# Seven half-size products for the second neighbour stage of a graph network's second layer, with the norms among the counts' products

## The chip, the core and the metric

The kernel runs on one core of a Trainium2 chip. The time is the device time of one execution in microseconds (us). PE is the tensor engine, DVE the vector engine, ACT the scalar engine, POOL the GpSimd engine; SP only issues DMAs here.

## What is computed

A graph of 625 nodes with 1024 features and 10000 edges goes through two layers. Layer 1 adds a two-step neighbour network (GraphSAGE) and a linear attention to x, then an attention with experts. The part that the change touches is the last line of the first block:

```python
def _sage_layer(h, edge_src, edge_dst, deg_inv, W_self, W_neigh, b):
    msg = h[edge_src]
    agg = segment_sum(msg, edge_dst, num_segments=h.shape[0])
    mean = agg * deg_inv[:, None]
    return h @ W_self + mean @ W_neigh + b
...
h = relu(_sage_layer(xn, src, dst, deg_inv, W_self0, W_neigh0, b0))
out = _sage_layer(h, src, dst, deg_inv, W_self1, W_neigh1, b1)
...
x = x + out + linear_attention(xn) @ L1_Wo + L1_bo
x = x + attention_and_experts(layernorm(x))
```

Everything is in f32. Written for the rows of one tile of nodes, the second step is x += h W_self1 + o L1_Wo + D^-1 C (h W_neigh1) + b. Here o is the linear attention's output before its last product, C the matrix of edge counts between nodes and D the in-degrees.

## The kernel before

The nodes are five tiles of 125 rows (`NT` = 5, `P` = 125), the features eight chunks of 128 (`KC` = 8). `hT` (two tiles of four chunks) and `oT` hold h and o with features on partitions, so that a matmul takes a 128x125 piece of them as its weights and streams 512 columns of a weight matrix. `group(dst, pairs)` (L137) sums a list of such matmuls in PSUM.

The order of every engine's work is written out by hand: `do(prep, pe, after)` emits first the `after` steps of the call before, then the PE work `pe`. Thus the evacuation of a product stands in the program behind the PE work that follows it, and each engine goes through its own list in that order.

Weights come in 1 MB tiles of 8 KB a partition from a pool of six buffers (`wpool`, tag "w"). `Half` loads one half of a matrix's columns (512) in two such tiles; `Quarter` loads 256 columns of a block in one. The loads stand in SP's queue in program order, and each waits until the buffer that it takes has been read for the last time.

The first step of the network (`quarter`, called as `p1` to `p3`) is already computed by Winograd's form of Strassen's scheme. A product of 2x2 blocks then takes seven block products instead of eight, with sums of blocks before (S1 to S4 of the left side, the mixes `third`, `second`, `first`, `fourth` of the weights) and after (u and u3). There [xn mean] is one side and [W_self0; W_neigh0] the other, in two quarters of 256 columns.

The second step is plain. For a half c of the columns, `neighbours(c)` makes z = h W_neigh1 for the five tiles (eight matmuls of 512 columns each, `pz`), and `split` writes it as a high part (rounded to fp32r, by ACT) and the rest (DVE). `last_of(t, c)` then makes, for a tile t, a group of sixteen matmuls (h W_self1 + o L1_Wo) and a group of ten counts' products in fp32r (C times both parts of z, five tiles of nodes each). DVE adds the two groups to x. The order is `neighbours(0)`, `last_of(0..4, 0)`, `neighbours(1)`, `last_of(0..4, 1)`.

Behind `last_of(t, 1)` stand `norm_rows(t - 1)`, the normalisation of a finished row of x (statistics, two square roots, `xs`), and `turn_rows(nxT, t - 2, 0)`, which transposes `xs` on PE and scales it into `nxT`. Tiles 3 and 4 are turned among the first key and query products of the next attention (`keys`, `q0`).

Of the kernel before, what the change touches and what calls it, by code (L numbers as in the profile page):

```python
# [20 lines left out]
NT = 5  # L21
# [32 lines left out]
def attempt(ctx: ExitStack, tc: tile.TileContext, w: dict, out: bass.AP, shifted: bool):  # L54
# [8 lines left out]
    def ps1(name):  # L63
        pool, n = psums[-1]
        return pool.tile([128, 512], FP, tag="ps1", name=name, bufs=n)
# [47 lines left out]
    class Half:  # L113


        def __init__(self, pool, src, c, tag="w", padded=None, now=True):
            v = src.rearrange("(k p) n -> p k n", p=128)
            self.parts = []

            def load():  # L120
                i = len(self.parts)
                t = pool.tile([128, 4, 512], FP, tag=tag, name="w", padded_shape=padded)
                self.parts.append(t)
                return nc.sync.dma_start(out=t, in_=v[:, 4 * i:4 * i + 4, c * 512:(c + 1) * 512])

            self.load = lambda: behind(load(), latest["pe"])
            if now:
                load()
                load()
# [4 lines left out]
    def group(dst, pairs):  # L134

        for i, (lhsT, rhs) in enumerate(pairs):
            made = nc.tensor.matmul(dst, lhsT=lhsT, rhs=rhs, start=(i == 0), stop=(i == len(pairs) - 1))  # L137
        latest["pe"] = made.ins.name

    class Quarter:  # L140


        def __init__(self, lo, *parts):
            self.tiles = {}
            self.source = {name: [(src, k, lo + 512 * (name[1] == "2")) for src, k in parts[int(name[0]) - 1]]
                           for name in ("11", "12", "21", "22")}

        def room(self, name):
            self.tiles[name] = wpool.tile([128, KC, 256], FP, tag="w", name="wq" + name)

        def load(self, *names):
            for name in names:
                self.room(name)
                at = 0
                for src, k, lo in self.source[name]:
                    n = k.stop - k.start
                    nc.sync.dma_start(out=self.tiles[name][:, at:at + n, :],
                                      in_=w[src].rearrange("(k p) n -> p k n", p=128)[:, k, lo:lo + 256])
                    at += n

        def mix(self, dst, a, b, op):
# [14 lines left out]
    def add(dst, a, b):  # L176
        nc.vector.tensor_tensor(dst, a, b, op=ALU.add)
# [19 lines left out]
    def nodes(t):  # L197
        return slice(t * P, (t + 1) * P)
# [1032 lines left out]
    def split(src, high, low):  # L1231

        nc.scalar.activation(high, src, AF.Copy)
        if not shifted:
            nc.vector.tensor_tensor(low, src, high.bitcast(FP), op=ALU.subtract)
# [38 lines left out]
    meanT = []  # L1274

    every = slice(0, KC)
    quarters = [Quarter(256 * i, [("W_self0", every)], [("W_neigh0", every)]) for i in range(2)]
    quarters[0].room("2")
    quarters[0].load("12", "21", "11", "22")
    for k in range(KC):  # L1280
# [38 lines left out]
    def four(f):  # L1319
        for j in range(2):  # L1320
            f(slice(4 * j, 4 * j + 4), meanT[j])
# [17 lines left out]
    def quarter(i):  # L1339
        q = quarters[i]  # L1340
        kept = {}
        u = spool.tile([128, 2, HN], FP, tag="u", name="u", bufs=2)
        u3 = spool.tile([128, 2, HN], FP, tag="u", name="u3", bufs=2)

        def product(name, right, after):
            def pe():
                kept[0] = ps2("pw")
                for a in range(2):
                    wt = q.tiles[name]
                    group(kept[0][:, a, :HN], [(wt[:, k, a * 128:(a + 1) * 128], right[k]) for k in range(KC)])  # L1350

            return lambda: do(None, pe, lambda: after(kept[0][:, :, :HN]))

        def done(c, h, a, b):
            dst = hT[c][:, 2 * i:2 * i + 2, h]
            add(dst, a, b)
            for a in range(2):
                m = 4 * c + 2 * i + a
                nc.scalar.activation(dst[:, a, :], dst[:, a, :], AF.Relu, bias=b0_t[:, m:m + 1])

        def both(p):
            done(1, tail, p, u3)
            add(u, p, u)

        return [product("11", A11, lambda p: nc.scalar.activation(u, p, AF.Copy)),
                product("21", A12, lambda p: done(0, head, p, u)),
                product("2", S2k, lambda p: add(u, p, u)),
                product("12", S3k, lambda p: add(u3, p, u)),
                product("21", A22, lambda p: done(0, tail, p, u3)),
                product("11", S1k, both),  # L1370
                product("22", S4k, lambda p: done(1, head, p, u))]

    now, then = quarters
    then.load("12")
    p1, p2, p6, p7, p4, p5, p3 = quarter(0)
    four(sum1)
    four(sum2)
    p1()
    p2()
    now.first()  # L1380
    four(sum3)
    p6()
    now.fourth()
    four(sum4)
    then.load("11")
    p7()
    then.load("22")
    p4()
    then.load("21")
    p5()  # L1390
    then.third()
    p3()
    then.room("2")
    p1, p2, p6, p7, p4, p5, p3 = quarter(1)
    p1()
    then.second()
    p2()
    then.first()
    p6()
    then.fourth()  # L1400
    nc.vector.tensor_tensor(b_t[0], b_t[0], b_t[1], op=ALU.add)
    p7()
    for t in range(2):
        nc.vector.tensor_tensor(x[:, t, :], x[:, t, :], b_t[0][:P], op=ALU.add)
    p4()
    for t in range(2, NT):
        nc.vector.tensor_tensor(x[:, t, :], x[:, t, :], b_t[0][:P], op=ALU.add)
    p5()
    p3()
    z, ws, wo = [], [], []  # L1410

    def neighbours(c):

        zc = big.tile([P, 2, NT, 512], NUM, tag="big", name="z")
        z.append(zc)
        wn1 = Half(wpool, w["W_neigh1"], c)
        ws.append(Half(wpool, w["W_self1"], c))
        wo.append(Half(wpool, w["L1_Wo"], c))
        for t in range(NT):
            def pe():  # L1420
                hold["pz"] = ps1("pz")
                group(hold["pz"][:P], [(hT[k // 4][:, k % 4, nodes(t)], wn1(k)) for k in range(KC)])

            def after(t=t):
                split(hold["pz"][:P], zc[:, 0, t, :], zc[:, 1, t, :])

            do(None, pe, after)

    neighbours(0)
    seven.close()  # L1430


# [26 lines left out]
    def norm_rows(t):  # L1459

        st = pool.tile([P, 2, 6], FP, tag="st", name="st", bufs=2)
        for h in range(2):
            nc.vector.bn_stats(st[:, h, :], x[:, t, h * 512:(h + 1) * 512])
        nc.vector.bn_aggr(mv2[:, t, :], st)
        rs, rr = rs2[:, t:t + 1], r1[:, t:t + 1]
        nc.scalar.activation(rs, mv2[:, t, 1:2], AF.Sqrt, bias=eps_ln[:P], scale=1.0)
        nc.vector.reciprocal(rs, rs)
        nc.vector.scalar_tensor_tensor(rr, mv2[:, t, 1:2], rs, rs, op0=ALU.mult, op1=ALU.mult)
        nc.scalar.activation(rr, rr, AF.Sqrt, bias=eps_6[:P], scale=1.0)
        nc.vector.reciprocal(rr, rr)  # L1470
        nc.vector.tensor_tensor(rr, rr, rs, op=ALU.mult)
        xs = hold["xs", t] = pool.tile([P, D], FP, tag="xs", name="xs", bufs=2)
        nc.vector.tensor_scalar(xs, x[:, t, :], mv2[:, t, 0:1], rr, op0=ALU.subtract, op1=ALU.mult)
# [2 lines left out]
        xs = hold.pop(("xs", t))  # L1476
        do(None, lambda: transpose_in(T, t, xs, lambda dst, src, h: by_gain(dst, src, which, h, P)))

    def last_of(t, c):
        def pe():  # L1480
            p = hold["px"] = ps2("px3")
            group(p[:P, 0, :], [(hT[k // 4][:, k % 4, nodes(t)], ws[c](k)) for k in range(KC)]
                  + [(oT[:, k, nodes(t)], wo[c](k)) for k in range(KC)])
            group(p[:P, 1, :], [(CTr[:, s, nodes(t)], z[c][:, i, s, :]) for i in range(1 if shifted else 2)
                                for s in range(NT)])

        def after():
            xc = x[:, t, c * 512:(c + 1) * 512]
            nc.vector.tensor_tensor(xc, hold["px"][:P, 0, :], xc, op=ALU.add)
            nc.vector.scalar_tensor_tensor(xc, hold["px"][:P, 1, :], dinvT[:, t:t + 1], xc,  # L1490
                                           op0=ALU.mult, op1=ALU.add)

        do(None, pe, after)

    for t in range(NT):
        last_of(t, 0)
    neighbours(1)
    for t in range(NT):
        last_of(t, 1)
        if t:  # L1500
            norm_rows(t - 1)
        if t > 1:
            turn_rows(nxT, t - 2, 0)


    kvc = mid([128, 2 * NP + NT * 256], "kvc")
# [36 lines left out]
                      kcT[:, a, :]) for a in range(2)]  # L1543
    q0 = [query(0, a) for a in range(2)]
    keys[0](0)
    turn_rows(nxT, NT - 2, 0)
    norm_rows(NT - 1)
    keys[1](0)
    q0[0](0)
    turn_rows(nxT, NT - 1, 0)  # L1550
    for t in range(3):
        value(t)
    keys[0](1)
# [639 lines left out]
```

## Time and profile before

| | us |
|---|---|
| median of 3 runs (2128.26 to 2129.67) | 2129.18 |
| the profiled execution, its own time | 2152.51 |
| its span, first to last instruction | 2150.7 |
| first `neighbours` matmul starts | 915.60 |
| first `last_of` matmul starts | 949.93 |
| second pass of `last_of` starts | 1064.51 |
| first key product of the next attention starts | 1148.79 |

PE is busy 2065.9 us of the span (96%), DVE 800.0 (37%), ACT 200.4 (9%), POOL 302.7 (14%). In a profile's row of a group, "x160" counts records: an f32 matmul is two records, an fp32r one is one. The first number behind the bar is the busy time of the group in us with overlaps counted once, the second the mean duration of one record in ns, and the last the idle time of the engine just before the group, with what ended it. Since matmuls overlap in the pipeline, the mean duration is longer than the time that one takes from its successor.

### The profile page before, as it was taken

The page shows a single profiled execution, that of the slowest core. Times are in us where ns is not written, and L with a number is a line of the kernel's source. Part 1 is how long each engine was busy: PE and PEld are TensorE (multiplying, and loading weights), DVE is VectorE, ACT ScalarE, POOL GpSimd, SP SyncE. Part 2 cuts the span into 40 slices and gives each one's busy share as a digit, 9 for nine tenths or more (in the row PEclk, how much of TensorE's full clock was granted, in tenths as well). Part 3 has the DMA queues.
Part 4 walks back from the last instruction along what each step waited for, and adds up shares of the span by engine and source line. Part 5 has one row for each costly group of instructions (what it writes and reads, how often), then busy time and mean ns, then how long its engine had stood idle before and what let it go on. Part 6 is the DMA issues. An engine that isn't in the chain of part 4 may idle for free. (4 is left out here: it accounts for less than half of the span.)

```text
span 2150.7 us, 17267 instructions
## 1 busy us (share of the span) xinstructions
PE 2065.9 (96%) x6806; PEld 1175.4 (55%) x6806; DVE 800.0 (37%) x1290; ACT 200.4 (9%) x369; POOL 302.7 (14%) x321
## 2 busy tenths in 40 slices
PE   8999999599899999999999999999999999999998
PEld 6555475255445787744456776457644444444443
DVE  5775568467532673210022234256311111111012
ACT  2100010012211100000000111111000000000000
POOL 1666656500000000100000000110000000000011
PEclk9999999799999999999999999999999999999999
DMA  7523254080122112410203201122589889987832
GB/s 217 201 91 108 79 178 136 22 229 24 39 88 79 39 40 73 148 64 16 101 0 108 79 1 39 30 79 98 197 327 329 299 298 329 329 315 265 305 130 83
DMA packets 156244, 301.61 MB, mean 140 GB/s; under 512 B 12539, under 2 KB 42114, under 8 KB 156150
## 3 DMA queue, kind: packets, MB, share of 16 engines
q1 hardware_dynamic: 135580, 251.50, 33.3%
q0 software_dynamic: 15584, 38.66, 5.7%
q10 hardware_dynamic: 4986, 10.22, 1.5%
q8 instruction: 57, 0.93, 0.2%
q14 instruction: 37, 0.30, 0.0%
HBM read 277.49 MB, written 22.84 MB: 140 GB/s over the span
## 5 line engine op out<-in xcount | busy, mean ns | idle before, releaser
L137 PE MATMUL pu<-w,xgT 128*128 128x512 f32 x768 | 333.9, 593 | 2.6 <-DVE xgT L1440 2.6
L137 PEld LDWEIGHTS pu<-w,xgT 128*128 128x128 f32 x768 | 144.0, 190 | 175.5 <-issue 172.2
L137 PE MATMUL pyb<-w,hb 128*128 128x512 f32 x384 | 174.3, 598 | 2.4 <-ACT yb L105 2.1
L137 PE MATMUL pk<-w,xnT 128*125 128x512 f32 x320 | 141.3, 593 | 3.9 <-ACT xnT L1104 2.2
L137 PE MATMUL pq<-xnT,w 128*128 128x313 f32 x512 | 139.2, 431 | 3.9 <-DVE v L332 3.9
L137 PE MATMUL pv<-w,xnT 128*125 128x512 f32 x320 | 140.8, 593 | 0.9 <-DVE x L986 0.9
L2027 DVE TENSOR_TENSOR su<-pu,su 128x512 f32<-128x512 f32 x24 | 16.6, 691 | 313.9 <-ACT su L2026 313.9
L137 PEld LDWEIGHTS pq<-xnT,w 128*128 128x128 f32 x512 | 97.9, 192 | 43.0 <-DVE v L332 4.7
L137 PEld LDWEIGHTS pyb<-w,hb 128*128 128x128 f32 x384 | 69.8, 189 | 90.9 <-issue 74.8
L805 PE MATMUL px<-w,oT 128*125 128x512 f32 x160 | 74.1, 619 | 27.7 <-DMA table<-es,at 22.5
L137 PEld LDWEIGHTS pk<-w,xnT 128*125 128x125 f32 x320 | 59.2, 187 | 75.6 <-issue 72.4
L137 PEld LDWEIGHTS pv<-w,xnT 128*125 128x125 f32 x320 | 59.4, 188 | 73.5 <-issue 71.2
L680 POOL DMA_INDIRECT table<-es,at x79 | 85.7, 1085 | 58.9 <-issue 35.0
L660 POOL DMA_INDIRECT ga<-xl_d,si x79 | 79.5, 1006 | 54.3 <-issue 25.9
L2010 POOL DMA_INDIRECT xg<-rows_d,slots x12 | 11.6, 970 | 507.9 <-PE pxg L2017 454.7
L660 POOL DMA_INDIRECT gb<-xr_d,di x79 | 77.2, 977 | 24.1 <-issue 22.9
L137 PE MATMUL px<-w,hT 128*125 128x512 f32 x160 | 70.3, 592 | 0.0
L137 PE MATMUL px<-w,oT 128*125 128x512 f32 x160 | 70.3, 592 | 0.0
L137 PE MATMUL pX<-w,aT 128*125 128x512 f32 x160 | 69.3, 592 | 0.0
L137 PE MATMUL pz<-w,hT 128*125 128x512 f32 x160 | 69.0, 592 | 0.0
L137 PE MATMUL pq<-nxT,w 128*128 128x313 f32 x256 | 68.7, 426 | 0.0
L137 PE MATMUL ph<-S,wq 128*128 128x313 f32 x256 | 68.7, 427 | 0.0
(385 smaller groups left out, 2535.5 us busy)
## 6 DMA issues: line engine op xcount, KB each, us to landing
w<-in_eW_dram SPq DMA_DIRECT2D x144, 1024.0 KB
w<-in_L_Wk_dram SPq DMA_DIRECT2D x8, 1024.0 KB
w<-in_L_Wv_dram SPq DMA_DIRECT2D x8, 1024.0 KB
w<-in_L_Wq_dram SPq DMA_DIRECT2D x8, 1024.0 KB
w<-in_L_Wo_dram SPq DMA_DIRECT2D x8, 1024.0 KB
wq<-in_sW_dram SPq DMA_DIRECT2D x16, 512.0 KB
table<-none SPq DMA_DIRECT2D x1, 6160.0 KB
y_d<-yb ACTq DMA_DIRECT2D x12, 512.0 KB
```

The costliest lines, as they stand in the source:

```text
L137: made = nc.tensor.matmul(dst, lhsT=lhsT, rhs=rhs, start=(i == 0), stop=(i == len(pairs) - 1))
L660: got = nc.gpsimd.indirect_dma_start(out=ab[g][side][0:p, j, :], out_offset=None, in_=src[:, :], in_offset=bass.IndirectOffsetOnAxis(ap=ix ...
L680: put = nc.gpsimd.indirect_dma_start(out=table[:, :], out_offset=bass.IndirectOffsetOnAxis(ap=at[0:p, lo + j:lo + j + 1], axis=0), in_=es[ ...
L805: made = nc.tensor.matmul(hold["px", t][:P, c, :], lhsT=oT[:, k, nodes(t)], rhs=wo[c](k), start=(k == 0), stop=(k == KC - 1 and keep is no ...
L2010: nc.gpsimd.indirect_dma_start(out=xg, out_offset=None, in_=rows_d[:, :], in_offset=bass.IndirectOffsetOnAxis(ap=slots[:, b:b + 1], axis=0))
L2027: nc.vector.tensor_tensor(su, pu[:, 0, :], su, op=ALU.mult)
```

## The change

The second step is remade in three parts.

1. `seven_products` is the old order of the seven products as a function, called four times: twice for the first step as before, and twice for the self and attention products of tiles 0 to 3. In these, [h o] is one side (tokens 0 to 249 and 250 to 499 as its two rows of blocks) and [W_self1; L1_Wo] the other, in quarters of 256 columns. Every product has two tiles of 125 tokens and eight chunks. Results are added to x by DVE.
2. z for tiles 0 to 3 is made by seven products too (`z_products`): h is split into two halves of its features, and the blocks of W_neigh1 are 512 by 512. The fifth tile's z is made by plain products (`z_last`).
3. The fifth tile's own self and attention products (`last_tile`) are plain, from W_self1 and L1_Wo loaded again in halves; `oT4` is a copy of o's last tile, since z takes oT's buffer. They stand among the counts' products (`of_neighbours`, now both halves of the columns of a tile together) and the norms and turns. Tile 4 comes before tiles 2 and 3.

The bias additions to x, which stood between products of the first step, stand there still.

```diff
+    quarters = [Quarter(256 * i, [(a, every)], [(b, every)]) for a, b in (("W_self0", "W_neigh0"), ("W_self1", "L1_Wo"))
+                for i in range(2)] + [Quarter(0, [("W_neigh1", front)], [("W_neigh1", back)], n=512)]
+
+    def seven_products(i, p1, p2, p6, p7, p4, p5, p3, between={}):
+        now, then = quarters[i], quarters[i + 1] if i + 1 < len(quarters) else None
...
+        if then:
+            then.load("12")
+        p1()
+        if i:
+            now.second()
+        other(1)
+        p2()
+        now.first()
+        other(2)
+        p6()
+        now.fourth()
+        other(6)
+        if then:
+            then.load("11")
+        p7()
+        other(7)
+        if then:
+            then.load("22")
+        p4()
+        other(4)
+        if then:
+            then.load("21")
+        p5()
+        if then and then.n == 256:
+            then.third()
+        other(5)
+        p3()
+        if then:
+            then.room("2")
...
-    z, ws, wo = [], [], []
-    def neighbours(c):
...
+    def on_tokens(name, left, wt, n, parts, after):
+        def pe():
+            p = hold[name] = ps2(name)
+            for j in range(2):
+                dst = p[:P, j, :] if n == 512 else p[:P, 0, 256 * j:256 * j + 256]
+                group(dst, [(left(k)[:, j * P:(j + 1) * P], wt()[:, k, :]) for k in range(parts)])
...
+    def rows_quarter(i):
...
+        return [product("11", h_(early), lambda p: nc.scalar.activation(u, p, AF.Copy)),
+                product("21", o_(early), lambda p: plus(at(0, 0), p, u)),
+                product("2", S_(S2), lambda p: add(u, p, u)),
+                product("12", S_(S3), p7),
+                product("21", o_(late4), lambda p: plus(at(0, 2), p)),
+                product("11", S_(S1), p5),
+                product("22", S_(S4), lambda p: plus(at(1, 0), p, u))]
...
+    seven_products(2, *rows_quarter(0), {1: [lambda: by_four(by_sum[0]), lambda: by_four(by_sum[1])],
+                                         2: [lambda: by_four(by_sum[2])], 6: [lambda: by_four(by_sum[3])]})
+    seven_products(3, *rows_quarter(1))
...
-    def last_of(t, c):
...
+    def z_last(c):
...
+    def z_products():
...
+        def done(c, rows, a, b):
+            got = pool.tile([P, 2, 512], FP, tag="zt", name="zt", bufs=1)
+            add(got, a, b)
+            split(got, z[c][:, 0, rows:rows + 2, :], z[c][:, 1, rows:rows + 2, :])
...
+    def of_neighbours(t):
         def pe():
             p = hold["px"] = ps2("px3")
-            group(p[:P, 0, :], [(hT[k // 4][:, k % 4, nodes(t)], ws[c](k)) for k in range(KC)]
-                  + [(oT[:, k, nodes(t)], wo[c](k)) for k in range(KC)])
-            group(p[:P, 1, :], [(CTr[:, s, nodes(t)], z[c][:, i, s, :]) for i in range(1 if shifted else 2)
-                                for s in range(NT)])
+            for c in range(2):
+                group(p[:P, c, :], [(CTr[:, s, nodes(t)], z[c][:, i, s, :]) for i in range(1 if shifted else 2)
+                                    for s in range(NT)])
...
-    for t in range(NT):
-        last_of(t, 0)
-    neighbours(1)
-    for t in range(NT):
-        last_of(t, 1)
-        if t:
-            norm_rows(t - 1)
-        if t > 1:
-            turn_rows(nxT, t - 2, 0)
+    def last_tile(c):
+        ws, wo = (Half(wpool, w[name], c) for name in ("W_self1", "L1_Wo"))
...
+    z_last(1)
+    wn1.third()
+    p1, p2, p6, p7, p4, p5, p3 = z_products()
+    p1()
+    wn1.second()
+    z_last(0)
...
+    p2()
+    wn1.first()
...
+    p6()
+    wn1.fourth()
+    p7()
+    p4()
+    final = [last_tile(0)]
+    p5()
+    p3()
+    final.append(last_tile(1))
+    of_neighbours(0)
+    of_neighbours(1)
+    norm_rows(0)
+    final[0]()
+    norm_rows(1)
+    of_neighbours(4)
+    turn_rows(nxT, 0, 0)
+    of_neighbours(2)
+    turn_rows(nxT, 1, 0)
+    norm_rows(2)
+    final[1]()
+    turn_rows(nxT, 2, 0)
+    of_neighbours(3)
+    norm_rows(4)
...
     keys[0](0)
-    turn_rows(nxT, NT - 2, 0)
-    norm_rows(NT - 1)
+    norm_rows(3)
+    turn_rows(nxT, 4, 0)
     keys[1](0)
     q0[0](0)
-    turn_rows(nxT, NT - 1, 0)
+    turn_rows(nxT, 3, 0)
```

More of the change, by code (lines that the diff above doesn't have):

```diff
@@ L140, in attempt, with __init__ @@
     class Quarter:
-        def __init__(self, lo, *parts):
+        def __init__(self, lo, *parts, n=256):
             self.tiles = {}
+            self.n = n
             self.source = {name: [(src, k, lo + 512 * (name[1] == "2")) for src, k in parts[int(name[0]) - 1]]
@@ L148, in room @@
         def room(self, name):
-            self.tiles[name] = wpool.tile([128, KC, 256], FP, tag="w", name="wq" + name)
+            self.tiles[name] = wpool.tile([128, 2048 // self.n, self.n], FP, tag="w",
+                                          name="wq" + name)
         def load(self, *names):
@@ L157, in load @@
                     nc.sync.dma_start(out=self.tiles[name][:, at:at + n, :],
-                                      in_=w[src].rearrange("(k p) n -> p k n", p=128)[:, k, lo:lo + 256])
+                                      in_=w[src].rearrange("(k p) n -> p k n", p=128)[:, k, lo:lo + self.n])
                     at += n
@@ L1276, in attempt, with other @@
     every = slice(0, KC)
-    quarters = [Quarter(256 * i, [("W_self0", every)], [("W_neigh0", every)]) for i in range(2)]
+    front, back = slice(0, 4), slice(4, KC)
+    quarters = [Quarter(256 * i, [(a, every)], [(b, every)]) for a, b in (("W_self0", "W_neigh0"), ("W_self1", "L1_Wo"))
+                for i in range(2)] + [Quarter(0, [("W_neigh1", front)], [("W_neigh1", back)], n=512)]
+    def seven_products(i, p1, p2, p6, p7, p4, p5, p3, between={}):
+        now, then = quarters[i], quarters[i + 1] if i + 1 < len(quarters) else None
+        def other(name):
+            for f in between.get(name, ()):
+                f()
+        if then:
[27 more added lines that the diff above has]
+            then.room("2")
     quarters[0].room("2")
@@ L1371, in quarter, with biases @@
                 product("22", S4k, lambda p: done(1, head, p, u))]
-    now, then = quarters
-    then.load("12")
-    p1, p2, p6, p7, p4, p5, p3 = quarter(0)
+    def biases(*ts):
+        if 0 in ts:
+            add(b_t[0], b_t[0], b_t[1])
+        for t in ts:
+            add(x[:, t, :], x[:, t, :], b_t[0][:P])
     four(sum1)
     four(sum2)
[L1378 to L1407, printed above, removed]
@@ L1408, in attempt @@
-    p5()
-    p3()
-    z, ws, wo = [], [], []
-    def neighbours(c):
[L1414 to L1418, printed above, removed]
-        for t in range(NT):
[L1420 to L1427, printed above, removed]
@@ L1429, in attempt @@
-    neighbours(0)
+    seven_products(0, *quarter(0), {2: [lambda: four(sum3)], 6: [lambda: four(sum4)]})
+    seven_products(1, *quarter(1), {6: [lambda: biases(0, 1)], 7: [lambda: biases(2, 3, 4)]})
+    seven.close()
+    seven = ExitStack()
+    spool = seven.enter_context(tc.tile_pool(name="rows", bufs=1, reuse_waits="tile"))
+    early, late4 = slice(0, 2 * P), slice(2 * P, 4 * P)
+    S1, S2 = (mid([128, KC, 2 * P], name) for name in ("S1", "S2"))
+    S3, S4 = (spool.tile([128, KC, 2 * P], FP, name=name) for name in ("S3", "S4"))
@@ new lines, in sub, with by_four, done @@
+    def sub(dst, a, b):
+        nc.vector.tensor_tensor(dst, a, b, op=ALU.subtract)
+    def by_four(f):
+        for j in range(2):
+            k = slice(4 * j, 4 * j + 4)
+            f(k, hT[j], oT[:, k, :])
+    def on_tokens(name, left, wt, n, parts, after):
+        def pe():
+            p = hold[name] = ps2(name)
+            for j in range(2):
+                dst = p[:P, j, :] if n == 512 else p[:P, 0, 256 * j:256 * j + 256]
+                group(dst, [(left(k)[:, j * P:(j + 1) * P], wt()[:, k, :]) for k in range(parts)])
+        def done():
+            p = hold[name]
+            after(p[:P] if n == 512 else p[:P, 0, :].rearrange("p (j n) -> p j n", j=2))
+        return lambda: do(None, pe, done)
@@ new lines, in rows_quarter, with at, plus, product @@
+    def rows_quarter(i):
+        q = quarters[2 + i]
+        u, u3 = (spool.tile([P, 2, 256], FP, tag="u", name=name, bufs=2) for name in ("u", "u3"))
+        def at(c, rows):
+            return x[:, rows:rows + 2, c * 512 + 256 * i:c * 512 + 256 * i + 256]
+        def plus(dst, *parts):
+            for part in parts:
+                add(dst, dst, part)
+        def product(name, left, after):
+            return on_tokens("pl", left, lambda: q.tiles[name], 256, KC, after)
+        def h_(tokens):
+            return lambda k: hT[k // 4][:, k % 4, tokens]
+        def o_(tokens):
+            return lambda k: oT[:, k, tokens]
+        def S_(S):
+            return lambda k: S[:, k, :]
+        def p7(p):
+            add(u3, p, u)
+            plus(at(0, 2), u3)
+        def p5(p):
+            plus(at(1, 2), p, u3)
+            add(u, p, u)
+        return [product("11", h_(early), lambda p: nc.scalar.activation(u, p, AF.Copy)),
[5 more added lines that the diff above has]
+                product("22", S_(S4), lambda p: plus(at(1, 0), p, u))]
@@ new lines, in attempt @@
+    by_sum = [lambda k, h, o: add(S1[:, k, :], h[:, :, late4], o[:, :, late4]),
+              lambda k, h, o: sub(S2[:, k, :], S1[:, k, :], h[:, :, early]),
+              lambda k, h, o: sub(S3[:, k, :], h[:, :, early], h[:, :, late4]),
+              lambda k, h, o: sub(S4[:, k, :], o[:, :, early], S2[:, k, :])]
+    seven_products(2, *rows_quarter(0), {1: [lambda: by_four(by_sum[0]), lambda: by_four(by_sum[1])],
+                                         2: [lambda: by_four(by_sum[2])], 6: [lambda: by_four(by_sum[3])]})
@@ L1477, in turn_rows, with pe @@
         do(None, lambda: transpose_in(T, t, xs, lambda dst, src, h: by_gain(dst, src, which, h, P)))
-    def last_of(t, c):
+    oT4 = pool.tile([128, KC, P], FP, name="oT4")
+    nc.scalar.activation(oT4, oT[:, :, nodes(4)], AF.Copy)
+    z = [big.tile([P, 2, NT, 512], NUM, tag="big", name="z") for c in range(2)]
+    S12, S34 = (mid([128, 2, 4, 2 * P], name) for name in ("S12", "S34"))
+    S1, S2, S3, S4 = (S[:, i] for S in (S12, S34) for i in range(2))
+    wn1 = quarters[4]
+    def z_last(c):
+        def pe():
+            hold["pz"] = ps1("pz")
+            group(hold["pz"][:P], [(hT[k // 4][:, k % 4, nodes(4)], wn1.tiles[f"{1 + k // 4}{1 + c}"][:, k % 4, :])
+                                   for k in range(KC)])
+        do(None, pe, lambda: split(hold["pz"][:P], z[c][:, 0, 4, :], z[c][:, 1, 4, :]))
@@ new lines, in z_products, with product, p5 @@
+    def z_products():
+        u, u3 = (pool.tile([P, D], FP, tag="xs", name=name, bufs=2).rearrange("p (j n) -> p j n", j=2)
+                 for name in ("u", "u3"))
+        def product(name, left, after):
+            return on_tokens("pz2", lambda k: left[:, k, :], lambda: wn1.tiles[name], 512, 4, after)
+        def done(c, rows, a, b):
+            got = pool.tile([P, 2, 512], FP, tag="zt", name="zt", bufs=1)
+            add(got, a, b)
+            split(got, z[c][:, 0, rows:rows + 2, :], z[c][:, 1, rows:rows + 2, :])
+        def p5(p):
+            done(1, 2, p, u3)
+            add(u, p, u)
+        return [product("11", hT[0][:, :, early], lambda p: nc.scalar.activation(u, p, AF.Copy)),
+                product("21", hT[1][:, :, early], lambda p: done(0, 0, p, u)),
+                product("2", S2, lambda p: add(u, p, u)),
+                product("12", S3, lambda p: add(u3, p, u)),
+                product("21", hT[1][:, :, late4], lambda p: done(0, 2, p, u3)),
+                product("11", S1, p5),
+                product("22", S4, lambda p: done(1, 0, p, u))]
@@ L1487, in after @@
         def after():
[L1488 to L1491, printed above, removed]
+            xt = x[:, t, :].rearrange("p (c n) -> p c n", c=2)
+            nc.vector.scalar_tensor_tensor(xt, hold["px"][:P], dinvT[:, t:t + 1], xt, op0=ALU.mult, op1=ALU.add)
         do(None, pe, after)
-    for t in range(NT):
-        last_of(t, 0)
@@ L1497, in attempt, with now, pe @@
-    neighbours(1)
-    for t in range(NT):
-        last_of(t, 1)
-        if t:
-            norm_rows(t - 1)
-        if t > 1:
-            turn_rows(nxT, t - 2, 0)
+    def last_tile(c):
+        ws, wo = (Half(wpool, w[name], c) for name in ("W_self1", "L1_Wo"))
+        def now():
+            def pe():
+                hold["pr"] = ps2("pr")[:, 0, :]
+                group(hold["pr"][:P], [(hT[k // 4][:, k % 4, nodes(4)], ws(k)) for k in range(KC)]
+                      + [(oT4[:, k, :], wo(k)) for k in range(KC)])
+            xc = x[:, 4, c * 512:(c + 1) * 512]
+            do(None, pe, lambda: add(xc, hold["pr"][:P], xc))
+        return now
@@ new lines, in attempt @@
+    add(S1, hT[0][:, :, late4], hT[1][:, :, late4])
+    sub(S2, S1, hT[0][:, :, early])
+    z_last(1)
[4 more added lines that the diff above has]
+    z_last(0)
+    sub(S3, hT[0][:, :, early], hT[0][:, :, late4])
+    p2()
+    wn1.first()
+    sub(S4, hT[1][:, :, early], S2)
+    p6()
[8 more added lines that the diff above has]
+    of_neighbours(1)
```

## The prediction

> **What bounds the kernel now.** I read the page's first two sections, then the waits of the tensor engine (PE) in the stretch that the change touches, then that stretch's groups and timeline.
>
> ```profile
> span 2150.7 us, 17267 instructions
> ...
> PE 2065.9 (96%) x6806; PEld 1175.4 (55%) x6806; DVE 800.0 (37%) x1290; ACT 200.4 (9%) x369; POOL 302.7 (14%) x321
> ...
> PEclk9999999799999999999999999999999999999999
> ```
>
> PE works 96% of the span. The stretch is 780 to 1210 us, at granted clock 1.00 in every window that I asked for, so microseconds taken from PE there are microseconds of the run if nothing new makes PE wait. It has two waits today:
>
> ```profile
> engine line waited for: us in total, times, longest us
> PE pkc L137 <- DVE nxT L1440: 1.3, 1, 1.3
> PE pvc L137 <- DVE nxT L1440: 0.3, 1, 0.3
> ```
>
> So the change is worth the difference in PE work, plus or minus waits. The groups of the stretch (780 to 1205 us) and four rows of its timeline give the prices:
>
> ```profile
> L137 PE MATMUL px<-w,hT 128*125 128x512 f32 x160 | 70.3, 592 | 0.0
> L137 PE MATMUL px<-w,oT 128*125 128x512 f32 x160 | 70.3, 592 | 0.0
> L137 PE MATMUL pz<-w,hT 128*125 128x512 f32 x160 | 69.0, 592 | 0.0
> L162 DVE TENSOR_TENSOR wq<-wq,wq 128x2048 f32<-128x2048 f32 x8 | 18.3, 2284 | 7.5 <-PE pw L137 7.5
> L137 PE MATMUL pvc<-wvc,nxT 128*125 128x256 f32 x80 | 17.7, 380 | 0.3 <-DVE nxT L1440 0.3
> L1324 DVE TENSOR_TENSOR S<-xnT,meanT 128x1252 f32<-128x1252 f32 x2 | 2.8, 1454 | 0.0
> ```
>
> ```profile
> 1163.76 10.62 PE L137 MATMUL pvc<-wvc,nxT 128*125 128x256 f32 x48 [0.34 <-DVE nxT L1440]
> 1174.22 0.95 PE L137 MATMUL pkc<-nxT,wkc 128*128 128x313 f32 x3
> 1195.31 7.07 PE L137 MATMUL pvc<-wvc,nxT 128*125 128x256 f32 x32
> 1202.21 0.95 PE L137 MATMUL psc<-qT,kvc 128*125 128x313 f32 x3
> ```
>
> A single matmul's 592 or 380 ns overlaps its neighbours; the price is start to start. Each f32 matmul stands as two records. At 512 columns, a tile's eight `pz` matmuls (16 records) start 6.87 us apart (the copies of z stand at 922.66 and 929.53): 0.429 us a record. At 256 columns, (1202.21 - 1195.31)/32 = 0.2156 and (1174.22 - 1163.76)/48 = 0.2179; I take 0.2165. A tile of `last_of` takes 16.04 us (1064.51 to 1080.54): 32 x 0.429 = 13.73 leaves 2.31 for ten records of counts, 0.231 each.
>
> **The change part by part.**
> *Self and attention products of tiles 0 to 3.* Removed: 4 tiles x 2 halves x 16 matmuls = 256 records of 512 columns, 256 x 0.429 = 109.8 us. Added: two quarters x 7 products x 2 tiles x 8 matmuls = 448 records of 256 columns, 448 x 0.2165 = 97.0 us. Gain 12.8.
> A rule speaks against this step. The Trainium skill, "TensorE: Matmul & The Clock Gate", section "Back-to-back issue gap", says that in a stream of weight loads and matmuls "the per-MM spacing is set by *both* ops"; it gives 81 ns for 128-column pairs against about 56 for the matmul alone. Adding those 25 ns to a 256-column pass (107 + 2.5) is 134 ns, 268 a two-pass record: 448 x 0.268 = 120 us, and the gain turns into a loss of 10 (an estimate from that page). The row of this trace has the same operands in kind (a 128x125 load for every 256-column matmul) at 0.2165, so the 188 ns load is covered. I take the row.
>
> *Neighbour products.* Removed: 160 `pz` records. Added: 7 products x 2 tiles x 4 matmuls x 2 = 112, and the fifth tile's plain 32. 144 x 0.429 = 61.8 against 68.6. Gain 6.9.
>
> *The fifth tile's plain products and the counts' products.* 64 records of 512 columns and 100 of counts stay as many; they only move. Gain 0, from -0.5 to +0.5 for changes of kind between neighbours.
>
> *Vector engine (DVE).* For each self quarter: four weight mixes at 2.28, and 11 additions of 512 columns, no dearer than the 0.69 of `x<-px,x`. The four sums are made once, in eight halves of 1000 columns; at the 1.454/1252 of L1324 that is 1.16 each. Together 2 x (9.1 + 7.6) + 9.3 = 43 us beside 97 of PE. The neighbour stage: 9.1 of mixes, 4.6 of sums, 1.4 for the fifth tile, and 11 passes of 1024 columns at the 1.22 of L986, some 28 us beside 62. I laid them out by product (6.9 us long in both stages): first self product from 0, the last hT addition ends at 1.1, the weight sum at 3.4, S1 at 5.8, S2 at 8.1; S2 and the sum are wanted at 13.8. The hT chunks that the last W0 product finishes (k 6 and 7) are through ACT at 1.8 and 2.3; the new first product reaches them at 2.6 and 3.0. Cost 0; if the cover is gone, the 0.8 us margin of k 6 is the first to break. The 14 evacuations lag by no more than one product, with three PSUM pairs in turn.
>
> *Loads.* 20 MB instead of 12: eight 256-column quarters of W_self1 and L1_Wo, four parts of W_neigh1, eight parts for the fifth tile. Each on SP's queue waits for a buffer: quarter "11" for the third product of the stage before, "22" for the fourth, "21" for the fifth. A 256-column load today: issued at 822.96, bytes until 827.3, so 4.4 us; a 512-column one is alike:
>
> ```profile
> 856.72 0.37 SPq L124 DMA_DIRECT2D w<-in_W_neigh_dram  x1
> ```
>
> ```profile
> 858.00:859.00 1.00, 1.00 (x6) 0.71 (x5) 1.00 (x1) 0.57 (x2) 0.00 (x0) 1.00 0.91 178
> 859.00:860.00 1.00, 1.00 (x6) 0.71 (x5) 0.74 (x1) 0.00 (x0) 0.00 (x0) 1.00 1.06 412
> 860.00:861.00 1.00, 1.00 (x5) 0.71 (x4) 0.00 (x0) 0.00 (x0) 0.00 (x0) 1.00 1.02 397
> 861.00:862.00 1.00, 1.00 (x5) 0.76 (x4) 0.00 (x0) 0.00 (x0) 0.00 (x0) 1.00 0.11 39
> ```
>
> The last two columns are the DMA share and GB/s. "21" is wanted three products (20.7 us) after its issue, "11" four; "22" is the tightest: its mix stands on DVE one product (6.9 us) later, ahead of the next evacuation, and DVE would hold that up by what the load is late. The fifth tile's last two parts are issued while its first half runs, over 20 us before their use. POOL's zero fill of y_d (bytes from 898 to 915 today) moves behind the fourth product of the second self quarter; W_neigh1's "22" is issued at the same moment and has 24 us until its use, "21" one product later with 31. Cost 0; were these the full 17 us late they would still be in time.
>
> *Neighbours to counts.* `last_of` began on old z; now the first counts' products want the z that the last product has just made: addition 1.22, ACT copy some 1.05, subtraction 1.22 in a row. PE reaches the high part after ten records, at 2.3 us, and it is there at 2.6; the low part is wanted five records on, at 3.8, ready at 3.9. Cost 0.4, with bounds 0 and 4 (none of the chain hidden).
>
> *Norms among the counts' products.* Tiles run 0, 1, fifth c=0, 4, 2, fifth c=1, 3. A norm takes 3.9 us on DVE from its statistics to xs (1154.92 to 1158.79); counted from the first counts' product, norms of tiles 0, 1, 2, 4, 3 end at about 10, 16, 40, 55 and 60, and their turns are due on PE at 28, 34, 48, 58 and 68. `keys[0](0)` no longer follows a turn directly: tile 2's nxT is written by 51, and 4.6 us of tile 3's counts' products put the keys at 54. The 1.3 us wait goes; the 0.3 stays. Gain 1.3, bounds -2 and 1.3.
>
> Sum: 12.8 + 6.9 + 1.3 - 0.4 = 20.6 us. The profiled execution took 2152.5 (span 2150.7), so 2131.9 there. It is 23 us slower than the median; the stretch ran at full clock, so I take the same microseconds off the median: 2129.2 - 20.6 = 2108.6.
>
> **The rivals.**
> *Small waits eat part of it.* 21 products with evacuations, mixes and sums in one DVE order: a stall of 0.5 us at each costs 10 and gives 2119. For: the order is written by hand, and DVE stands at the head of its queue waiting for loads and products. Against: today's stage of the same pattern has none:
>
> ```profile
> 797.00:865.00 68.00, 68.00 (x262) 48.99 (x261) 26.31 (x21) 4.71 (x9) 0.00 (x0) 1.00 0.19 62
> ```
>
> There PE is busy 68.00 of 68.00 with DVE at 26.31. New products last 6.9 us where those last 8.4, so the load on DVE is a little higher. 0.13.
> *Slower: the weight load shows.* If a load that changes for every 256-column matmul were only half covered, a record would cost 0.2165 + 0.094 = 0.31, the self stage 139.1 instead of 109.8, and the run 2129.2 + 29.3 - 6.9 - 1.3 + 0.4 = 2150.7. It decides at (20.6/448 = 0.046 more) 0.262 us a record. For: the quoted rule, and 188 ns of load under 216 of matmul is a thin cover. Against: 80 records of the same form, no idle but the 0.3. 0.04.
> *Nothing left.* The self stage neither gains nor loses (0.245 a record) and a few waits of 7 us eat the rest: 2129. For it only the two rivals together. 0.03.
> *The gain is larger.* The smaller pitch (0.2156 throughout), no wait at the counts: 2107.8; anything lower needs a change outside the stretch, where the instruction order is the same. 0.03 for under 2104.
>
> **How the numbers follow.** Forecast 0.77, rivals 0.13, 0.04, 0.03, 0.03. The predicted time is the forecast's, 2109. The range goes from 2104 (below the smaller pitch by the spread of runs and some luck) to 2115 (the counts' chain uncovered, 4, and the key wait's bound); half of the small-wait cases lie above it. 0.2% is 4.3 us, about what a measurement of this kernel can tell from no change. Faster by more: 0.93. Within: 0.03. Slower by more: 0.04.
>
> **What would show it.** Groups `pl` with 448 records at some 97 us busy (0.2165 each, mean near 380 ns), `pz2` and `pz` together 144; no wait of PE in the self and neighbour stages above 0.5 us, one of about 0.4 on z before the first counts' products, no `pkc` wait on nxT. From the end of the last W0 product to the first `pkc` about 212 us against 232 (915.60 to 1147.5). I am wrong if `pl` starts are more than 0.23 apart, if PE waits in total over 4 us there on wq, S or z, or if time changes outside.

## The result, and the profile after

The changed kernel took 2112.11 us (median of 6 runs, 2106.05 to 2118.55) against 2130.6 before (6 runs, 2128.26 to 2132.94): ratio 0.9915, 95% interval 0.9895 to 0.9935. That is 18.5 us less. Timed again among the experiments it took 2109.12 against 2131.18, ratio 0.9897 (0.9878 to 0.9916), 22.1 us less. The forecast was 20.6 less. The first interval stands for 14 to 22 us, the second for 18 to 26. The runs' spread is wider than the differences that matter here, so the working below is checked in the profiles, where a stretch of a few hundred microseconds repeats within some tenths.

From the page of the changed kernel, the rows shown of the one before:

```profile
span 2109.1 us, 17713 instructions
...
PE 2037.1 (97%) x6982; PEld 1207.8 (57%) x6982; DVE 855.6 (41%) x1326; ACT 203.1 (10%) x369; POOL 303.0 (14%) x321
...
PEclk9999999799999999999999999999999999999999
```

The two profiled spans differ by 41.6 us, twice what the timed runs do. One difference of the two traces tells why: the first product of the network's first step, where nothing has been changed yet, starts at 797.46 in the trace before and at 777.1 here, and from 773.0 to 778.0 in the eight kernels of the experiments. So 20.4 us of the 41.6 belong to that one execution of the kernel before, and to the front of the kernel. In that front PE was idle for 14.5 us that the list of waits puts down to "issue", that is, to nothing that the profile shows; the nine profiles of the changed kernel and its variants have 1.9 us of it at most. What it came from stays open. From that product to the end, 1353.2 us have become 1332.0.

The waits of PE from the first new product on (890 to 1180 us):

```profile
engine line waited for: us in total, times, longest us
PE pvc L137 <- DVE nxT L1511: 0.3, 1, 0.3
```

The key products' 1.3 us wait is gone, and no product of the two new stages is in the list. PE's groups between 890 and 1110 us (records, busy us, mean ns):

```profile
L137 PE MATMUL pl<-wq,S 128*125 128x256 f32 x256 | 55.9, 379 | 0.0
L137 PE MATMUL pz<-wq,hT 128*125 128x512 f32 x80 | 34.7, 592 | 0.0
L137 PE MATMUL pl<-wq,oT 128*125 128x256 f32 x128 | 28.3, 379 | 0.0
L137 PE MATMUL pz<-wq,S 128*125 128x512 f32 x64 | 27.8, 592 | 0.0
L137 PE MATMUL px<-z,CT 125*125 125x512 f32 x100 | 25.1, 405 | 0.1
L137 PE MATMUL pl<-wq,hT 128*125 128x256 f32 x64 | 14.1, 379 | 0.0
```

`pl` has 448 records and `pz` (which takes in `pz2`; the trace leaves a name's number out) 144. And the windows from the first self product to z, to the counts' products, to the first key product (columns: length, busy time of PE, weight loads, DVE, ACT, POOL, granted clock, DMA share, GB/s):

```profile
895.30:991.90 96.60, 96.60 (x449) 84.02 (x448) 41.12 (x38) 3.13 (x5) 7.52 (x12) 1.00 0.33 115
991.90:1053.30 61.40, 61.40 (x144) 26.83 (x144) 24.81 (x19) 5.39 (x6) 0.66 (x2) 1.00 0.24 86
1053.30:1107.40 54.10, 54.00 (x190) 32.99 (x189) 23.87 (x46) 4.70 (x10) 0.00 (x0) 1.00 0.52 174
```

The edges of these windows are rounded. Measured from start to start the three are 96.69, 61.40 and 54.06 us, 212.15 in all. In the kernel before, the same work stands between the first `neighbours` matmul and the first key product:

```profile
915.60:1148.79 233.19, 231.89 (x605) 111.03 (x603) 36.80 (x69) 10.61 (x21) 0.62 (x1) 1.00 0.17 59
```

The stretch gives 21.0 us, the whole of the gain within 0.2.

### The profile page after: what moved, and what is told of

It reads as the page before. It is cut to its first block, busy times and chain, and to the rows that moved or that the text cites. A ratio compares the mean times of both kernels' runs of the same rounds, so it can differ in the third digit from the quotient of the medians.

```text
span 2109.1 us, 17713 instructions
## 1 busy us (share of the span) xinstructions
PE 2037.1 (97%) x6982; PEld 1207.8 (57%) x6982; DVE 855.6 (41%) x1326; ACT 203.1 (10%) x369; POOL 303.0 (14%) x321
## 5 line engine op out<-in xcount | busy, mean ns | idle before, releaser
L807 PE MATMUL px<-w,oT 128*125 128x512 f32 x160 | 71.7, 606 | 30.9 <-DMA table<-es,at 27.8
L807 PEld LDWEIGHTS px<-w,oT 128*125 128x125 f32 x160 | 30.3, 192 | 69.9 <-issue 36.3
L164 DVE TENSOR_TENSOR wq<-wq,wq 128x2048 f32<-128x2048 f32 x28 | 63.9, 2283 | 12.8 <-PE pw L137 7.5
L398 DVE RECIPROCAL z<-z 128x626 f32<-128x626 f32 x16 | 65.1, 4066 | 0.6
```

The lines of the kernel that those rows point to most:

```text
L164: nc.vector.tensor_tensor(self.tiles[dst], self.tiles[a], self.tiles[b], op=op)
L398: nc.vector.reciprocal(z, z)
L807: made = nc.tensor.matmul(hold["px", t][:P, c, :], lhsT=oT[:, k, nodes(t)], rhs=wo[c](k), start=(k == 0), stop=(k == KC - 1 and keep is no ...
```

## The experiments

"Stage" is the first window above, "stretch" all three; both are given from start to start. Single profiled executions are compared by these; the whole run is given where it was timed several times.

**Again, beside the next three.** The changed kernel, not edited.

> The changed kernel as it is, beside the next three. If the gain lies wholly in the stretch of the change, the stretch (first self product to first key product) is 212.1 us again within 0.3, whatever the whole run does; the run is 18 to 21 us under the kernel before. If part of the gain is in the front of the kernel, the stretch or the time up to the first W0 product of the first step (777 in the changed kernel's profile, 797 in the one before) moves with the run.

The stretch was 212.2 us (891.9 to 1104.1), the first product of the first step stood at 773.7, the run at 2109.12, 22.1 under the kernel before where 18 to 21 was expected. Between the two profiles of this kernel the span differs by 3.3 us, the start of that first product by 3.4 and the stretch by less than 0.1: here the front moves and the changed part repeats.

**Eight products at half width.**

The edit, shortened (`t` is one of the product's two tiles, `c` the half of the columns):

```diff
-    seven_products(2, *rows_quarter(0), {1: [...], 2: [...], 6: [...]})
-    seven_products(3, *rows_quarter(1))
+    # for each quarter: four groups of 16 matmuls, 256 columns
+    group(p[:P, 0, 256 * j:256 * j + 256],
+          [(hT[k // 4][:, k % 4, t], q.tiles[f"1{1 + c}"][:, k, :]) for k in range(KC)]
+          + [(oT[:, k, t], q.tiles[f"2{1 + c}"][:, k, :]) for k in range(KC)])
```

> Undoes the seven products of the self and attention part, but keeps their half width: eight plain products of 256 columns, 512 records, no sums and no mixes. PE's price by record: 512 x 0.2156 = 110.4 us instead of 96.6, the stretch 13.8 longer, so half the width by itself costs 0.6 against the 109.8 of 512-column products. Rival (vector engine or waits pace the products): without 34 us of sums and mixes the stage is no longer than about 100. Rival (weight loads show at half width): over 125.

The three windows of this kernel:

```profile
891.20:1001.70 110.50, 110.50 (x514) 96.14 (x513) 7.93 (x10) 1.93 (x3) 0.62 (x1) 1.00 0.20 67
1001.70:1063.10 61.40, 61.40 (x146) 26.89 (x144) 24.12 (x18) 5.39 (x6) 0.00 (x0) 1.00 0.24 86
1063.10:1117.10 54.00, 53.90 (x190) 32.98 (x189) 23.84 (x46) 4.70 (x10) 0.00 (x0) 1.00 0.51 175
```

The stage is 110.5 us, 13.8 longer, and nothing else has moved. DVE went from 41.12 us busy to 7.93, and PE took longer: so DVE was not what paced the stage. The run took 2122.84 (ratio to before 0.997, 0.9956 to 0.9984), 13.7 more than the changed kernel beside it. Half width alone costs 0.7 against 256 records at 0.429; the gain of this part is the eighth product.

**Plain products for z.**

```diff
-    p1, p2, p6, p7, p4, p5, p3 = z_products()
...
+    for t in range(NT):
+        z_plain(1, t)
+    for t in range(3):
+        z_plain(0, t)
     final = [last_tile(0)]
...
+    for t in range(3, NT):
+        z_plain(0, t)
     final.append(last_tile(1))
```

> Undoes the seven products of z alone: ten plain tiles of eight 512-column matmuls from the same four tiles of W_neigh1. By record: 160 x 0.4265 = 68.2 us instead of 61.4, the stretch 6.8 longer. Rival (the chain from the last seven-product to the counts' products matters): the chain is shorter here, copy and subtraction of one tile of 512 columns, and up to 0.5 comes back, so 6.3.

z lasted 68.3 us (992.77 to 1061.03), 6.9 more, and the tail 53.6 instead of 54.1: the stretch is 218.5 (896.1 to 1114.6), 6.4 above the 212.2. That is the figure with the shorter chain. The run: 2118.59, ratio 0.994 (0.9923 to 0.9957). The chain can be seen in the first counts' products. First the changed kernel (in the run "again"), then this one (start, length, group):

```profile
1049.98 10.30 PE L137 MATMUL px<-z,CT 125*125 125x512 f32 x40
```

```profile
1061.03 9.85 PE L137 MATMUL px<-z,CT 125*125 125x512 f32 x40
```

The same 40 records take 0.45 us longer behind the seven products. The list of waits has no row for it on PE. The weight loads of the changed kernel ("again") show where it lies: they stop once for the high part of z, which ACT copies, and once for the low part, which DVE subtracts.

```profile
1052.95 0.99 PEld L137 LDWEIGHTS px<-z,CT 125*125 125x125 f32 x5 [0.54 <-ACT z L1235]
1054.21 1.92 PEld L137 LDWEIGHTS px<-z,CT 125*125 125x125 f32 x9 [0.27 <-DVE z L1237]
```

With plain z the first of these stops is 0.20 and the second is not there.

**The old order of the tail.**

```diff
...
+    final[0]()
+    final[1]()
+    for t in range(NT):
+        of_neighbours(t)
+        if t:
+            norm_rows(t - 1)
+        if t > 1:
+            turn_rows(nxT, t - 2, 0)
...
-    norm_rows(3)
-    turn_rows(nxT, 4, 0)
+    turn_rows(nxT, 3, 0)
+    norm_rows(4)
...
-    turn_rows(nxT, 3, 0)
+    turn_rows(nxT, 4, 0)
```

> Keeps all products and undoes the order alone: the fifth tile's products first, then the counts' products of tiles 0 to 4 one after the other with norms and turns between as in the kernel before. Counts' products of both halves last 4.6 us and a turn 1.0, but the vector engine needs 1.3 + 3.9 + 1.3 = 6.5 us for each tile, so it falls behind by 0.9 a tile: the first key product waits about 3.9 us for nxT, the stretch is 216. Rival (the order is worth only the wait of before): 1.3, the stretch 213.4.

```profile
1102.85 1.01 PE L212 MATMUL ptr<-ident,xs 125*128 125x125 f32 x8
1107.18 7.21 PE L137 MATMUL pkc<-nxT,wkc 128*128 128x313 f32 x16 [3.31 <-DVE nxT L1511]
```

These two rows of its timeline follow each other on PE: after the last turn it waits 3.31 us for nxT. The stretch was 215.2 (892.0 to 1107.2), 3.0 above the changed kernel, 0.8 short of the expectation. Two sizes were off: DVE's period for a tile is 6.15 us (statistics start at 1089.17, 1095.32, 1101.47), not 6.5, and the fifth tile's products, now in front, cover the 0.45 of z's chain.

The stretch ends too early to hold the whole cost. Behind the wait, the first sixteen records of keys take 7.04 us up to the next turn at a granted clock of 0.61; in the changed kernel ("again", the second row) they take 4.21 at 1.00:

```profile
1107.18:1114.22 7.04, 7.04 (x16) 4.69 (x17) 0.53 (x1) 0.00 (x0) 0.00 (x0) 0.61 0.20 78
1104.06:1108.27 4.21, 4.21 (x17) 2.97 (x16) 3.46 (x7) 0.54 (x2) 0.00 (x0) 1.00 0.70 251
```

So the wait of 3.3 us cost 2.8 more after its end. From the first self product to that turn it is 222.2 against 216.4. The run: 2114.02, ratio 0.9923 (0.9903 to 0.9942), 4.9 more than the changed kernel beside it. With counts' products packed this closely the order is worth 5.9 us by the profile and some 5 by the runs, not the 1.3 that it removed from the kernel before. There the clock stayed at 1.00 behind the wait of 1.3 us.

**Half the width again.**

```diff
-                dst = p[:P, j, :] if n == 512 else p[:P, 0, 256 * j:256 * j + 256]
-                group(dst, [(left(k)[:, j * P:(j + 1) * P], wt()[:, k, :]) for k in range(parts)])
+                for lo in (0, 128) if n == 256 else (0,):
+                    dst = p[:P, j, :] if n == 512 else p[:P, 0, 256 * j + lo:256 * j + lo + 128]
+                    group(dst, [(left(k)[:, j * P:(j + 1) * P], wt()[:, k, lo:lo + 128] if n == 256 else wt()[:, k, :])
+                                for k in range(parts)])
```

> The self and attention products with every 256-column matmul cut into two of 128 columns: 896 records, the same columns in all. By the trace's row of 128x129 records (pkv, 160 in 19.7 us busy) 0.123 us a record: 110 us instead of 96.6, the stretch 13.6 longer. By the page's 81 ns for a 128-column pair, twice for two passes, 0.162: 145 us, 48.6 longer. If the 188 ns of a weight load bounded the pitch: 168 us, 72 longer.

```profile
893.90:992.30 98.40, 98.22 (x897) 97.87 (x896) 41.21 (x38) 3.13 (x5) 7.50 (x12) 1.00 0.33 113
```

None of the three prices was right; the 81 ns of the second is the figure of the Trainium skill that the prediction quotes. 896 records took 98.5 us, 0.110 each, only 1.8 us more than half as many of twice the width. The weight loads are busy 97.87 of 98.40, back to back although each is 188 ns long: loads overlap one another too. The matmuls' columns alone account for the pace. From 512 to 256 columns a record goes from 0.429 to 0.2158, so 128 columns fewer again should leave 0.109, and each product but the first runs at 0.109 (6.99 us for 64 records). The first takes 7.66, since one wait appeared:

```profile
PE pl L137 <- ACT hT L1401: 0.2, 1, 0.2
```

This is the hT of the last W0 product. Its narrow groups reach chunk 6 in half the time, and the margin of 0.8 us that the prediction named as the first to break did break. It cost 0.7 us of the 1.8, though the list shows 0.2.

**More work on the vector engine.** `spare` is a buffer that nothing else uses. The second kernel has six additions instead of two.

```diff
+            def more(p):
+                after(p)
+                for _ in range(2):
+                    add(spare, x[:, 0, :], x[:, 1, :])
...
-            return on_tokens("pl", left, lambda: q.tiles[name], 256, KC, after)
+            return on_tokens("pl", left, lambda: q.tiles[name], 256, KC, more)
```

> Two idle additions of 1024 columns (1.22 us each) on the vector engine behind every evacuation of the self and attention products, 34 us more in that stage (41 before, of 96.6). If the vector engine has the slack that its layout shows (every sum and mix due more than 4 us after it is made), PE does not wait: stage 96.6. Rival (evacuations nearly pace the products): each of 14 products 1 to 2.4 longer, 110 to 130.

```profile
893.90:990.60 96.70, 96.70 (x450) 84.08 (x449) 71.79 (x64) 2.20 (x4) 7.53 (x12) 1.00 0.34 115
```

DVE is busy 71.79 of the stage's 96.70 us and PE 96.70: no wait. The stretch is 212.2, as without them.

> Six such additions behind every evacuation, 102 us more: the vector engine's own time is 143.6, over PE's 96.6. It must now pace the stage, less what it may lag at the end (three PSUM pairs, two products, 14 us): 130 to 144, the stretch 33 to 47 longer less what the neighbour stage takes up.

```profile
PE pl L137 <- DVE wq L164: 18.4, 3, 9.8
PE pl L137 <- ACT u L1493: 3.3, 1, 3.3
```

```profile
892.30:940.60 48.30, 44.93 (x208) 38.78 (x207) 46.88 (x40) 1.60 (x3) 0.00 (x0) 1.00 0.24 76
940.60:1016.40 75.80, 57.51 (x243) 48.32 (x242) 74.05 (x65) 0.60 (x1) 7.51 (x12) 0.89 0.28 97
```

The stage became 124.0 us and the stretch 240.3, 28.1 longer: DVE is the bound, as it should be, but by less than the 33 to 47 expected. The lag that I allowed it, 14 us, was too small: its last idle addition starts at 1038.2, 22 us behind the stage's end, taken up by the neighbour stage. What PE waited for is a weight mix three times of four (18.4 of 21.7 us), not a PSUM buffer. And 5.7 of the stage's 27.3 us more are in no wait: in the second window the granted clock is 0.89. These are the products behind the four waits:

```profile
923.50 7.14 PE L137 MATMUL pl<-wq,oT 128*125 128x256 f32 x32 [3.37 <-DVE wq L164]
954.66 8.86 PE L137 MATMUL pl<-wq,oT 128*125 128x256 f32 x32 [3.30 <-ACT u L1493]
973.28 15.65 PE L137 MATMUL pl<-wq,S 128*125 128x256 f32 x64 [9.76 <-DVE wq L164]
994.16 8.54 PE L137 MATMUL pl<-wq,oT 128*125 128x256 f32 x32 [5.22 <-DVE wq L164]
```

Without a wait, 32 records are shown as 7.07 us and 64 as 13.98. The first of the four lost nothing, and the clock was 1.00 in it. The other three lost 1.5 to 1.8 us each; the clock was 0.68 in the first 5.3 us behind the second wait, 0.76 in the first 6.7 us behind the third and 0.83 over the 8.4 us behind the fourth. So a wait of PE can cost twice, once as a wait and once as a slower clock behind it, and the length alone doesn't tell when: 3.37 us did not, 3.30 did. What decides was not tested.

**Another tail.** The new order in full, up to the next attention:

```python
final[0]()
of_neighbours(0)
of_neighbours(1)
norm_rows(0)
of_neighbours(2)
norm_rows(1)
turn_rows(nxT, 0, 0)
final[1]()
norm_rows(2)
turn_rows(nxT, 1, 0)
of_neighbours(4)
turn_rows(nxT, 2, 0)
of_neighbours(3)
norm_rows(4)
```

> All products of the changed kernel; only the order of the tail is new: the fifth tile's first half product stands right behind the last product of z, then the counts' products of tiles 0, 1, 2, its second half as cover for the norms, tiles 4 and 3 last. If the 54.1 us of the tail hold a hidden wait of the first counts' products for z (plain z gave 53.6), the tail is 53.6 and the stretch 211.7. If the wait isn't there, 212.2. The run itself can hardly show 0.5 us.

The stretch was 211.7 (896.1 to 1107.8): the 0.5 us are there and this order hides them. The run took 2111.33, ratio to before 0.9901 (0.9878 to 0.9924). By its timed runs it is the changed kernel's equal.

## Why the prediction was right

It was right in the time and in its steps; some sizes were off by tenths. The timed runs alone could not show that: with 18.5 and 22.1 us they do not tell 20.6 from 19 or 22. The stretch and the parts undone one by one do.

- **Self and attention products: 12.8 forecast.** By the changed kernel's own stage 109.8 - 96.7 = 13.1; undone at half width, 13.8. The pitch came out at 0.2158 us a record, close to the smaller of the two that the trace before gave (0.2156); I had gone between them.
- **The rule against it.** The Trainium skill's figure for a stream of 128-column pairs ("TensorE: Matmul & The Clock Gate", "Back-to-back issue gap": 81 ns) would have made the step a loss. At 256 columns the trace before already had the row that decided. At 128 columns "narrow" measured 0.109 us a record, 55 ns a pass if a record is two passes, as my estimate took it: near the 56 that the page gives for the matmul alone. No run here counts passes; a 512-column record of f32 takes 0.429, one of fp32r 0.231. The measurement decides: for these f32 streams the loads are hidden even there.
- **z: 6.9 forecast, 6.9 measured** by undoing it (160 records for 144).
- **z's chain: 0.4 forecast, 0.45 to 0.5 measured**, by two experiments that remove it in different ways. What was wrong is only where I said it would show: it is no wait of PE in the list, and shows in the weight loads.
- **The norms: 1.3 forecast**, and the wait is gone. What the order itself is worth depends on what it is compared with: against the old order with the new products it is 3.0 in the stretch and 2.8 in the slower clock behind it, a cost that neither the prediction nor the expectation had.
- **DVE and loads: 0 forecast.** DVE was busy 41.1 us in the stage (43 forecast) and 24.8 in the neighbour stage (28). The rows of the timeline after the last W0 product stand within half a microsecond of where they were laid out. Counted from the stage's start at 895.25, the last hT addition ends at 1.0 (forecast 1.1), the weight sum at 3.2 (3.4), S1 at 5.4 (5.8), S2 at 7.7 (8.1), and S2 is first read at 13.8:

```profile
895.25 7.07 PE L137 MATMUL pl<-wq,hT 128*125 128x256 f32 x32
895.45 0.81 DVE L179 TENSOR_TENSOR hT<-pw,u 128x626 f32<-128x626 f32 x1 [6.92 <-PE pw L137]
896.18 2.28 DVE L164 TENSOR_TENSOR wq<-wq,wq 128x2048 f32<-128x2048 f32 x1
...
898.38 2.30 DVE L179 TENSOR_TENSOR S<-hT,oT 128x1000 f32<-128x1000 f32 x2
900.60 2.30 DVE L1435 TENSOR_TENSOR S<-S,hT 128x1000 f32<-128x1000 f32 x2
...
909.06 13.98 PE L137 MATMUL pl<-wq,S 128*125 128x256 f32 x64
```

  The tightest load, "22" of the next quarter, is issued at 923.07, and the mix that needs it starts at 930.59, at once behind the evacuation before it: it was there. That it still had room is not shown: a load that is really late was not tried.
- **The sum.** 20.6 forecast, 21.0 in the stretch, 18.5 and 22.1 in the two timings. The parts as measured, 13.1 + 6.9 + 1.3 - 0.45, make 20.9. The forecast's 232 us for the kernel before end at 1147.5, where PE runs out of work; the first key product starts 1.3 later, so the stretch of before is 233.2. Of the rivals, the small waits did not come (21 products without one), and the visible weight load is excluded down to a quarter of the width that the kernel had.
- **The profile against the median.** Taking the same microseconds off both was right for the median and wrong for the profiled span (2131.9 forecast, 2111.03 taken): the 23 us by which that execution was slow did not come again. The step assumed that they would. Nine other profiles, all of the changed kernel and its variants, show no such excess; a second one of the kernel before was not taken.

## What to carry to other kernels

Where PE is busy all the time, a scheme that trades one product of eight for vector work paid here what PE's record count says, as long as the vector work of each product fitted within it and its results were due a product or two later. Lay out the one place where stages meet (here the last hT, 0.8 us) and the one chain that faces PE at the end (here z to the counts' products, 0.5). Price a narrower matmul by the start-to-start distance in the trace, not by its shown duration or by the weight load's. To judge a change of 1% whose runs spread by 0.6%, compare the stretch, and undo one part at a time. Let the stretch end behind the first work after a wait, not at its start: a wait of 3.3 us on PE cost another 2.8 in the records behind it.

## What the runs showed of the hardware that I had not expected

- An f32 matmul of 128 columns with a new 128x125 weight load each time ran at 0.109 us a record, with weight loads that the trace shows as 188 ns long. With 0.2158 at 256 columns and 0.429 at 512, the three lie on one line.
- PE's granted clock fell behind some waits of 3 to 10 us and not behind others: 0.61 over 7.0 us after one of 3.31 (old order of the tail), 0.68, 0.76 and 0.83 over 5 to 8 us after 3.30, 9.76 and 5.22 (six extra additions), but 1.00 after one of 3.37. In the stage it was 1.00 in all other runs.
- A wait on single records inside a run of matmuls is shown as a longer run (10.30 us for 9.85), not as a wait of PE; the weight loads show it as stops of 0.54 and 0.27.
